# One exponentiated state instead of two: its turned copy by 32 x 32 blocks and DRAM, logits in four column groups

## The chip, the cores and the metric

The kernel runs on 1 core of one Trainium2 chip. The metric is the device time of one execution in microseconds (us); lower is better. All data are fp32.

## The reference

The input x has 8 sequences of 256 tokens of 256 features (2048 tokens). The layer is x + attention(LN(x)) + FFN(LN(x)). The attention works with 16 heads of 128 and, per head, M = 64 states per token:

```
s   = clip(hs @ Ws1.T @ Ws2.T + bs2, -32, 32)      # [token, head, 64]
z   = cumlogsumexp(s, over tokens)
es  = exp(s);  enz = exp(-z)
A   = causal(q @ k.T * scale)                      # q, k with rotary positions
ok  = enz * (A @ es)                               # [token, 64]
qv  = softmax(ok)
W2  = causal((qv * enz) @ es.T)
o   = W2 @ v
out = (rmsnorm(o) * g_norm * silu(g)) @ Wo.T
```

es is thus contracted twice: over tokens in `A @ es` (the logits), and over states in `(qv * enz) @ es.T` (the weights). The FFN unpacks 4-bit weights (2048 x 256 three times) and computes down(gelu(gate) * up).

## The kernel before, in words

The work is cut into 32 steps: 4 groups of 512 tokens (two sequences; `TC` = 4 blocks of 128) times 8 pairs of heads. A step n is a pipeline stage: in loop turn n the kernel makes states, q and k of step n + 1, values, gates, scores, logits and softmax of step n, weights and outputs of step n - 1, and in every second turn `close` (the product with w_o) of steps n - 2 and n - 1. One bank of FFN work (`feeding`) is put in at evenly spread places, 4 or 5 a turn, and decoding of packed FFN weights (24 parts) by the list `DUE`.

The order on TensorE (PE) is written by hand: `POS` gives each piece its place within a turn, `START` other places for turns -1 and 0, `FEED` the stretch in which turn -1 gets FFN work. The pieces call their matmuls at once. What the other engines do with the results is a generator (`chain`) that names its engine and a cost at each `yield`; a planner (`advance`) issues the chains' instructions in the order of its own clocks, lowest `rank` first among equals, and `need` makes it issue all that a piece depends on. So the order on VectorE (DVE), ScalarE (ACT), GpSimd (POOL) and the DMA queue of SyncE (SP) is fixed when the program is built. PSUM has eight banks (`bank`).

Before, `states(n)` makes the states of a head pair twice on PE, in four row groups of 32 partitions (17 of them used: 16 ranks and a row of ones for the bias): four matmuls give [token, state] (tile es, L532), two of 256 columns give [state, token] (tile esT, L537). DVE clips both (L549), ACT exponentiates both (L555), and DVE makes enz from esT by a scan (L560) and a reciprocal (L566). es serves `logits` (L675, a head's 64 states in each of two column groups) and `cross` (L746, es with the values of a sequence's first half); esT serves `weights` (L771). `apply` (L799) puts cross into the outputs' banks.

Some results have to change from [token, feature] to [feature, token]. `turned` does that for ok and the softmax (tile ok to okT) and for the outputs (og to ogT): DVE transposes 32 x 32 blocks (L472), four DMAs on SP write them to a DRAM tile by_way (L476), and one reads them back (L485).

Other lines that are spoken of: rope L579 (PE), L589/L590 (ACT copies z), L592 (DVE), L594/L595 (POOL, tiles z, q and k); values and gates L636; scores L655/L658 with mask L646; ok from the logits' bank L686; maximum L707, exponentials L718, prT L729 (POOL); wt L781; outputs L815, their squares L828, L833, power L837, og L841; close L865; FFN gate L395, up L417, down L442, with L402 to L426 between them; decoding L349, L353, L355; norm L252 to L270; scaling of w_o by the norm's weight L495 (POOL); warm-up matmuls L879.

Of the kernel before, what the change touches and what calls it, by code (L numbers as in the profile page):

```python
# [10 lines left out]
F32 = mybir.dt.float32  # L11
I32 = mybir.dt.int32
# [15 lines left out]
SCALE = DK ** -0.5  # L28
GELU_C = 0.7978845608028654
GELU_A = 0.044715  # L30
WARM = 18


POS = {'scores': (0.053, 0.063),
 'logits': (0.14,),
 'softmax': (0.301,),
 'cross': (0.15,),
 'weights': (0.169,),
 'low': (0.046,),
 'states': (0.167,),  # L40
 'outputs': (0.364, 0.472),
 'close': (0.348, 0.396),
 'rope': (0.197, 0.336, 0.411, 0.543),
 'vg': (0.502, 0.663, 0.838, 0.869)}
START = {-1: {'states': (0.437,), 'rope': (0.128, 0.358, 0.518, 0.588)},
 0: {'vg': (0.0, 0.03, 0.076, 0.214),
     'scores': (0.082, 0.162),
     'states': (0.386,),
     'logits': (0.216,),
     'softmax': (0.433,),  # L50
     'rope': (0.211, 0.24, 0.245, 0.458)}}
FEED = {-1: (0.244, 1.0)}
NORMS = {0: 1, 2: 2, 5: 3}
NORM_AT = (0.204, 0.465)
FIRST = [0.29, 1.5]
LAST = [1.49, 1.82]
DUE = [4, 6, 7, 7, 8, 9, 10, 11, 11, 11, 12, 13, 14, 15, 15, 16, 17, 17, 18, 19, 19, 22, 23, 23, 24]


@with_exitstack  # L60
def layer_kernel(ctx: ExitStack, tc: tile.TileContext, a: dict, out: bass.AP):
# [40 lines left out]
    def S(n):  # L102
        return "s", 0.15 + 0.00088 * n

    def pe(t):

        clock["pe"] += t
# [32 lines left out]
    def new(pool, shape, tag, bufs=1, dtype=F32):  # L140

        users = held.setdefault(tag, [])
        if len(users) >= bufs:
            while any(c in chains for c in users[-bufs]):
                advance()
            floor[0] = max([floor[0]] + [c.at for c in users[-bufs]])
        t = pool.tile(shape, dtype, tag=tag, name=tag, bufs=bufs)
        users.append([])
        at_tag[id(t)] = t, users[-1]
        return t  # L150
# [8 lines left out]
    def chain(gen, *tiles, rank=1, at=0.0):  # L159


        c = Chain()
        c.rank = rank
        c.gen, c.at, c.what = gen, max(clock["pe"] + 0.2, floor[0], at), next(gen)
        floor[0] = 0.0
        chains.append(c)
        for t in tiles:
            at_tag[id(t)][1].append(c)
        return c

    def bank():
        t = new(ps_p, [P, 512], "ps", 8)
        clock["pe"] = max(clock["pe"], floor[0])
        floor[0] = 0.0
        return t
# [8 lines left out]
    nhalf = const.tile([P, TC], F32, tag="nhalf", name="nhalf")  # L184
    turns = const.tile([P, 2, T], F32, tag="turns", name="turns")
    cos, sin = turns[:, 0], turns[:, 1]

    small = const.tile([P, 258], F32, tag="small", name="small")
    w_s1 = small[:, 0:256].rearrange("p (c f) -> p c f", c=2)
# [297 lines left out]
        )  # L487

    def load_wo():
        for h in range(0, H, 4):  # L490
            nc.sync.dma_start(out=w_o[:, h : h + 4, :], in_=a["wo"][:, h : h + 4, :])

    def scale_wo(h):

        nc.gpsimd.tensor_scalar(  # L495
            w_o[:, h : h + 4, :], w_o[:, h : h + 4, :], gw, 0.5, ALU.mult, ALU.mult
        )

    def low_rank(g):

# [16 lines left out]
    def states(n):  # L517

        g, hp = steps[n]
        ms = slice(hp * P, (hp + 1) * P)  # L520
        (rT, c), to = rTs[g], of[n]
        need(c)
        es = to["es"] = new(p2, [P, TC, P], "es", 2)
        esT = to["esT"] = new(p2, [P, G], "esT", 2)

        pss = [bank() for _ in range(4)]
        toks, sts = [rT[32 * r : 32 * r + 17] for r in range(4)], [w_s2[32 * r : 32 * r + 17, ms] for r in range(4)]
        for i in range(2):
            for r, ps in enumerate(pss):
                if r < 2:  # L530
                    k = 2 * r + i
                    nc.tensor.matmul(  # L532
                        ps[:, i * P : (i + 1) * P], lhsT=toks[r][:, k * P : (k + 1) * P],
                        rhs=sts[r], start=True, stop=True,
                    )
                elif i == 0:
                    nc.tensor.matmul(  # L537
                        ps[:, 0:T], lhsT=sts[r], rhs=toks[r][:, (r - 2) * T : (r - 1) * T],
                        start=True, stop=True,
                    )  # L540

        enz = to["enz"] = new(p2, [P, G], "enz", 2)

        def work():
            flat = es.rearrange("p i m -> p (i m)")
            for t, r in ((esT, 2), (flat, 0)):
                yield "v", 0.8
                for k in range(2):
                    nc.vector.tensor_scalar(  # L549
                        t[:, k * T : (k + 1) * T], pss[r + k][:, 0:T], CLAMP, -CLAMP,  # L550
                        ALU.min, ALU.max,
                    )
            for t in (esT, flat):
                yield S(512)
                nc.scalar.activation(t, t, AF.Exp)  # L555
            for b in range(2):
                yield "v", 0.75
                e = esT[:, b * T : (b + 1) * T]

                nc.vector.tensor_tensor_scan(  # L560
                    enz[:, b * T : (b + 1) * T], e, e, 0.0, ALU.add, ALU.max
                )
            for i in range(TC):
                yield "v", 0.93
                r = enz[:, i * P : (i + 1) * P]
                nc.vector.reciprocal(r, r)  # L566

        pe(0.8)
        to["states"] = chain(work(), *pss, es, esT, enz)

    def rope(n, j, which):

# [93 lines left out]
    def logits(n):  # L666

        to = of[n]
        need(to["at", 0][1], to["at", 1][1], to["states"])
        es, enz = to["es"], to["enz"]  # L670
        ps = bank()
        for b in range(2):
            for c, q0 in ((0, 0), (1, P)):
                for j in range(2):
                    nc.tensor.matmul(  # L675
                        ps[j * M : (j + 1) * M, b * T + q0 : (b + 1) * T],
                        lhsT=es[:, 2 * b + c, j * M : (j + 1) * M],
                        rhs=to["at", j][0][b][:, 2 * c * P : 2 * c * P + T - q0],
                        start=c == 0, stop=c == 1,
                    )  # L680
        ok = new(p1, [P, 4, TC, 32], "ok")
        okT = to["okT"] = new(p1, [P, 4, TC, 32], "okT")

        def work():
            yield V(512)
            nc.vector.tensor_tensor(  # L686
                ok.rearrange("p c i k -> p i c k"), ps.rearrange("p (i c k) -> p i c k", i=TC, c=4),
                enz.rearrange("p (i c k) -> p i c k", i=TC, c=4), ALU.mult,
            )
            yield from turned(okT, ok)  # L690

        pe(1.4)
        to["logits"] = chain(work(), ps, ok, okT, enz, rank=0)
# [43 lines left out]
    def cross(n):  # L737


        to = of[n]  # L740
        need(*(to["v", i] for i in (0, 2)))
        es, v = to["es"], to["v"]
        ps = bank()
        for b in range(2):
            for j in range(2):
                nc.tensor.matmul(  # L746
                    ps[j * M : (j + 1) * M, b * DK : (b + 1) * DK],
                    lhsT=es[:, 2 * b, j * M : (j + 1) * M],
                    rhs=v[:, 2 * b, j * DK : (j + 1) * DK], start=True, stop=True,
                )  # L750
        z = new(p1, [P, 2 * DK], "cross")

        def work():
            yield S(256)
            nc.scalar.copy(z, ps[:, 0 : 2 * DK])

        pe(0.55)

        to["cross"] = z, chain(work(), ps, z)
# [96 lines left out]
    def close(n, i):  # L856

        g, hp = steps[n]
        ogT = [of[m]["ogT", j] for m in (n - 1, n) for j in range(2)]
        need(*(c for _, c in ogT))  # L860
        pst = bank()
        ps = pst.rearrange("p (i d) -> p i d", i=2)
        for k in range(2):
            for hh in range(4):
                nc.tensor.matmul(  # L865
                    ps[:, k, :], lhsT=ogT[hh][0][:, i + k],
                    rhs=w_o[:, (hp // 2) * 4 + hh, :], start=hh == 0, stop=hh == 3,
                )
        pe(1.73)
        chain(add_to(g * TC + i, ps), pst)  # L870
# [98 lines left out]
def _layout(x):  # L969
# [11 lines left out]
    def quarters(spread, of):  # L981
# [8 lines left out]
    n = {k: np.asarray(v) for k, v in x.items()}  # L990
    at, ff = "L0_attn_", "L0_ffn_"
    ws1 = n[at + "Ws1"].T.reshape(P, 2, 1, 16)
    ws1 = np.pad(ws1, [(0, 0)] * 3 + [(0, 16)]).repeat(4, 2).reshape(P, 256)
    bias = (np.arange(P) % 32 == 16).astype(np.float32).reshape(P, 1)
    ws2 = np.concatenate([n[at + "Ws2"].T, n[at + "bs2"].reshape(1, H * M)])
    ws2 = np.pad(ws2, [(0, 15), (0, 0)])
    return {
        "x": c(n[at + "hidden_states"].reshape(NG, 4, 4, 32, D).swapaxes(1, 2).reshape(NTOK, D)),
        "wqkvg": pairs([n[at + w] for w in ("Wq", "Wk", "Wv", "Wg")]),
        "wo": c(n[at + "Wo"].T.reshape(H, DK, D).transpose(1, 0, 2)),  # L1000
        "small": c(np.concatenate([ws1, bias, n[at + "g_norm_weight"].reshape(DK, 1)], 1)),
        "ws2": c(np.concatenate([ws2] * 4)),
        "codes": quarters(lambda w: w, "_W_packed"),
        "scales": quarters(lambda w: w.repeat(16, 0), "_scales"),
        "turns": c(np.concatenate([cos, sin], 1)),
# [19 lines left out]
```

## Time and profile before

| | |
|---|---|
| median of 3 runs | 1224.25 us (1223.51 to 1225.16) |
| the profiled execution's own time | 1225.03 us |
| its span | 1223.3 us |
| mean granted TensorE clock | 0.993 |
| DMA | 118.52 MB, 97 GB/s in the mean; the program's queue took 35.1% of 16 engines' span |

The span runs from the first to the last instruction; the rest of the execution's time lies around it. In the profile PE stands for matmuls and PEld for weight loads, which overlap them; an fp32 matmul is recorded as two MATMUL instructions. In the groups by line, the columns are: engine, operation, output <- inputs, shapes, count | busy time and mean ns of one | idle time of the engine just before them, and what ended it. In the list of waits they are: total us, times, longest us.

### The profile page before, as it was taken

The numbers are of one execution on the slowest core, as the hardware profiler recorded it, in microseconds if no ns is written. First come the engines' busy times: TensorE is split into PE (matmuls) and PEld (weight loads), VectorE is DVE, ScalarE is ACT, GpSimd is POOL, SyncE is SP. The second block draws the span as 40 slices with busy tenths as digits, with TensorE's granted clock in tenths as the row PEclk, the third lists the DMA queues.
The fourth block names the chain that finished last, engine by engine and source line by source line (L and its number), as shares of the span: only waits on it lengthen the run. The fifth ranks groups of instructions, "written<-read, shape, count | busy, mean of one in ns | idle before, by whom it ended". The sixth has DMA issues, their size and how long they took to land.

```text
span 1223.3 us, 18297 instructions
## 1 busy us (share of the span) xinstructions
PE 1191.8 (97%) x6076; PEld 841.9 (69%) x6076; DVE 905.0 (74%) x1739; ACT 511.4 (42%) x1641; POOL 483.2 (40%) x439
## 2 busy tenths in 40 slices
PE   9889799999999999999999999999999999999997
PEld 6456576666767667677776677776766767667675
DVE  6978768988477787866877776987776677676743
ACT  3433435435354443534444344444344454443431
POOL 4424544334344343444442344443234443343411
PEclk9989899999999999999999999999999999999999
DMA  5344542343343143333333333423233332334321
GB/s 185 87 121 121 130 112 63 102 129 104 87 104 106 45 117 96 104 96 94 85 90 90 99 104 104 103 56 101 70 104 95 95 80 69 100 98 117 84 76 52
DMA packets 120030, 118.52 MB, mean 97 GB/s; under 512 B 18688, under 2 KB 91520, under 8 KB 119936
## 3 DMA queue, kind: packets, MB, share of 16 engines
q1 hardware_dynamic: 119936, 117.36, 35.1%
q8 instruction: 48, 0.79, 0.3%
q14 instruction: 46, 0.38, 0.1%
HBM read 80.09 MB, written 37.22 MB: 96 GB/s over the span
## 4 chain that ended last, share of the span: by engine, by line
PE 85%; DVE 10%; POOL 2%; ACT 1%; issue 1%; DMA 1%; SPq 0%; DVEq 0%; POOLq 0%
PE ps L579 16%; PE ps L636 16%; PE ps L442 9%; PE ps L865 9%; PE ps L395 8%; PE ps L417 8%; PE ps L815 4%; PE ps L655 4%; PE ps L675 3%; PE ps L771 2%; PE ps L658 2%; DVE enz L566 1%; DVE esT L549 1%; PE ps L746 1%; PE ps L532 1%
## 5 line engine op out<-in xcount | busy, mean ns | idle before, releaser
L594 POOL TENSOR_TENSOR z<-z,turns 128x512 f32<-128x512 f32 x128 | 164.4, 1284 | 242.3 <-ACT z L590 235.6
L579 PE MATMUL ps<-xT,wts 128*128 128x512 f32 x512 | 241.8, 599 | 5.7 <-DVE t L410 1.6
L636 PE MATMUL ps<-wts,xT 128*128 128x256 f32 x1024 | 234.7, 379 | 1.0 <-DVE k L592 1.0
L636 PEld LDWEIGHTS ps<-wts,xT 128*128 128x128 f32 x1024 | 193.5, 190 | 52.3 <-issue 24.2
L579 PEld LDWEIGHTS ps<-xT,wts 128*128 128x128 f32 x512 | 93.6, 190 | 91.5 <-issue 77.2
L442 PE MATMUL ps<-w_down,inter 128*128 128x256 f32 x512 | 121.0, 390 | 8.8 <-DVE inter L426 4.2
L404 POOL TENSOR_SCALAR t<-t 128x512 f32<-128x512 f32 x64 | 40.0, 624 | 209.8 <-ACT t L402 207.8
L417 PE MATMUL ps<-xT,w_up 128*128 128x512 f32 x256 | 121.6, 597 | 0.0
L395 PE MATMUL ps<-xT,w_gate 128*128 128x512 f32 x256 | 120.7, 594 | 0.5 <-DVE sgate L624 0.5
L718 ACT ACTIVATE ok<-okT,mx 128x64 f32<-128x64 f32 x256 | 85.6, 337 | 81.5 <-DVE mx L712 80.3
L442 PEld LDWEIGHTS ps<-w_down,inter 128*128 128x128 f32 x512 | 98.9, 196 | 28.9 <-DVE inter L426 5.6
L589 ACT COPY z<-ps 64x512 f32<-64x512 f32 x128 | 74.6, 583 | 104.5 <-PE ps L579 98.7
L865 PE MATMUL ps<-w_o,ogT 128*128 128x256 f32 x512 | 115.6, 379 | 0.0
L595 POOL TENSOR_TENSOR q<-q,z 128x512 f32<-128x512 f32 x64 | 81.8, 1278 | 82.8 <-DVE q L592 59.8
L865 PEld LDWEIGHTS ps<-w_o,ogT 128*128 128x128 f32 x512 | 96.7, 190 | 21.3 <-issue 9.3
L566 DVE RECIPROCAL enz<-enz 128x128 f32<-128x128 f32 x128 | 108.1, 905 | 0.0
L370 DVE TENSOR_TENSOR res<-ps,res 128x512 f32<-128x512 f32 x64 | 43.8, 685 | 78.4 <-PE ps L442 42.5
L841 DVE SCALAR_TENSOR_TENSOR og<-ps,ss,sgate 128x128 f32<-128x128 f32 x256 | 73.5, 342 | 37.7 <-POOL ss L837 37.7
L837 POOL TENSOR_TENSOR ss<-ss,nhalf 128x4 f32<-128x4 f32 x64 | 64.9, 1017 | 68.6 <-DVE ss L833 66.5
L595 POOL TENSOR_TENSOR k<-k,z 128x512 f32<-128x512 f32 x64 | 82.9, 1295 | 20.9 <-DVE k L592 15.7
L408 ACT ACTIVATE t<-t 128x512 f32<-128x512 f32 x64 | 40.2, 629 | 121.2 <-DVE t L406 121.1
L646 DVE TENSOR_TENSOR at<-ps,mask 128x384 f32<-128x384 f32 x128 | 66.1, 551 | 32.7 <-PE ps L658 31.8
(80 smaller groups left out, 1919.7 us busy)
## 6 DMA issues: line engine op xcount, KB each, us to landing
wts<-in_wqkvg_dram SPq DMA_DIRECT2D x64, 512.0 KB, 4.4
by_way<-ok SPq DMA_DIRECT2D x256, 64.0 KB, 1.8
okT<-by_way SPq DMA_DIRECT2D x64, 256.0 KB, 2.7
by_way<-og SPq DMA_DIRECT2D x256, 64.0 KB, 2.0
ogT<-by_way SPq DMA_DIRECT2D x64, 256.0 KB, 4.0
pk<-in_codes_dram SPq DMA_DIRECT2D x12, 256.0 KB, 3.7
sc<-in_scales_dram SPq DMA_DIRECT2D x12, 256.0 KB, 3.6
w_o<-in_wo_dram SPq DMA_DIRECT2D x4, 512.0 KB, 5.6
```

The costliest lines, as they stand in the source:

```text
L395: nc.tensor.matmul(pg, lhsT=w_gate[:, c, ns], rhs=xT[:, c, gs], start=c == 0, stop=c == 1)
L417: nc.tensor.matmul(pu, lhsT=w_up[:, c, ns], rhs=xT[:, c, gs], start=c == 0, stop=c == 1)
L442: nc.tensor.matmul(ps[:, k, :], lhsT=inter[g, n][0][:, (i + k) * P : (i + k + 1) * P], rhs=w_dn[:, n, :], start=n == 2 * q, stop=n == 2 * ...
L566: nc.vector.reciprocal(r, r)
L579: nc.tensor.matmul(ps, lhsT=w[:, c, :], rhs=xT[:, c, g * G : (g + 1) * G], start=c == 0, stop=c == 1)
L589: nc.scalar.copy(z[0:64], pv[64:128])
L594: nc.gpsimd.tensor_tensor(z, z, sin_b, ALU.mult)
L595: nc.gpsimd.tensor_tensor(y, y, z, ALU.add)
L636: nc.tensor.matmul(ps[:, k, :], lhsT=xT[:, c, tt], rhs=w[:, which, c, :], start=c == 0, stop=c == 1,)
L718: nc.scalar.activation(pr[:, js, i, :], okT[:, js, i, :], AF.Exp, bias=mx[:, k : k + 1], scale=SCALE, accum_out=sm[:, k : k + 1],)
L841: nc.vector.scalar_tensor_tensor(og[:, :, k, :], po[:, k, :].rearrange("p (c k) -> p c k", c=4), ss[:, k : k + 1], sg[:, k, j * DK : (j + ...
L865: nc.tensor.matmul(ps[:, k, :], lhsT=ogT[hh][0][:, i + k], rhs=w_o[:, (hp // 2) * 4 + hh, :], start=hh == 0, stop=hh == 3,)
```

## The change

`states` makes only [state, token], with two matmuls in two row halves of 64 partitions (17 used in each). ScalarE writes the exponential twice, once in blocks of 32 into a tile `u` (shared with decoding) and once in place; the first goes through `turned` to es. `logits` and `cross` take es in four column groups of 32 states. `w_o` is scaled by chains of rank 2 that the planner places, and `close` needs them. Three warm-up matmuls fewer are run, and places and due times differ. Cut to its core:

```diff
-WARM = 18
-POS = {'scores': (0.053, 0.063),
+WARM = 15
+POS = {'scores': (0, 0.089),
- 'softmax': (0.301,),
+ 'softmax': (0.366,),
- 'outputs': (0.364, 0.472),
- 'close': (0.348, 0.396),
- 'rope': (0.197, 0.336, 0.411, 0.543),
- 'vg': (0.502, 0.663, 0.838, 0.869)}
-START = {-1: {'states': (0.437,), 'rope': (0.128, 0.358, 0.518, 0.588)},
+ 'outputs': (0.319, 0.427),
+ 'close': (0.396, 0.407),
+ 'rope': (0.178, 0.317, 0.392, 0.524),
+ 'vg': (0.502, 0.64, 0.838, 0.869)}
+START = {-1: {'states': (0.488,), 'rope': (0.221, 0.424, 0.53, 0.684)},
...
-     'states': (0.386,),
+     'states': (0.445,),
-     'rope': (0.211, 0.24, 0.245, 0.458)}}
-FEED = {-1: (0.244, 1.0)}
+     'rope': (0.24, 0.245, 0.249, 0.458)}}
+FEED = {-1: (0.055, 1.0)}
-LAST = [1.49, 1.82]
-DUE = [4, 6, 7, 7, 8, 9, 10, ..., 19, 19, 22, 23, 23, 24]
+LAST = [1.51, 1.82]
+DUE = [4, 6, 6, 7, 9, 9, 10, ..., 19, 19, 23, 23, 23, 24]
...
     def scale_wo(h):
-        nc.gpsimd.tensor_scalar(
-            w_o[:, h : h + 4, :], w_o[:, h : h + 4, :], gw, 0.5, ALU.mult, ALU.mult
-        )
+        def work():
+            yield "g", 1.15
+            nc.gpsimd.tensor_scalar(
+                w_o[:, h : h + 4, :], w_o[:, h : h + 4, :], gw, 0.5, ALU.mult, ALU.mult
+            )
+        scaled.append(chain(work(), rank=2, at=landed["wo"]))
...
-        pss = [bank() for _ in range(4)]
...
+        pss = [bank() for _ in range(2)]
+        for b, ps in enumerate(pss):
+            rows = slice(64 * b, 64 * b + 64)
+            nc.tensor.matmul(
+                ps[:, 0:T], lhsT=w_s2[rows, ms], rhs=rT[rows, b * T : (b + 1) * T],
+                start=True, stop=True,
+            )
...
+        u = new(de, [P, 2, CH], "u", 2, I32)
+        eb = u.bitcast(F32).rearrange("p k (x i y) -> p (k x) i y", i=TC, y=32)
+        es = to["es"] = new(p2, [P, 4, TC, 32], "es", 2)
+        def clipped():
+            yield "v", 0.8
+            for b in range(2):
+                nc.vector.tensor_scalar(
+                    esT[:, b * T : (b + 1) * T], pss[b][:, 0:T], CLAMP, -CLAMP, ALU.min, ALU.max
+                )
+            yield S(512)
+            nc.scalar.activation(
+                eb.rearrange("p c i k -> p i c k"),
+                esT.rearrange("p (i c k) -> p i c k", i=TC, c=4), AF.Exp,
+            )
+        def swapped():
+            yield first
+            yield from turned(es, eb)
+        def summed():
+            yield first
+            yield S(512)
+            nc.scalar.activation(esT, esT, AF.Exp)
...
-        pe(0.8)
-        to["states"] = chain(work(), *pss, es, esT, enz)
+        pe(0.65)
+        first = chain(clipped(), *pss, esT, u)
+        to["es_at"] = chain(swapped(), es, u)
+        to["states"] = chain(summed(), esT, enz)
...
         # logits; cross in the same way
-                for j in range(2):
+                for r in range(4):
                     nc.tensor.matmul(
-                        ps[j * M : (j + 1) * M, b * T + q0 : (b + 1) * T],
-                        lhsT=es[:, 2 * b + c, j * M : (j + 1) * M],
-                        rhs=to["at", j][0][b][:, 2 * c * P : 2 * c * P + T - q0],
+                        ps[32 * r : 32 * (r + 1), b * T + q0 : (b + 1) * T],
+                        lhsT=es[:, r, 2 * b + c, :],
+                        rhs=to["at", r // 2][0][b][:, 2 * c * P : 2 * c * P + T - q0],
...
         # close
-        need(*(c for _, c in ogT))
+        need(*(c for _, c in ogT), *scaled)
```

More of the change, by code (lines that the diff above doesn't have):

```diff
@@ L55 @@
 FIRST = [0.29, 1.5]
-LAST = [1.49, 1.82]
-DUE = [4, 6, 7, 7, 8, 9, 10, 11, 11, 11, 12, 13, 14, 15, 15, 16, 17, 17, 18, 19, 19, 22, 23, 23, 24]
+LAST = [1.51, 1.82]
+DUE = [4, 6, 6, 7, 9, 9, 10, 11, 11, 11, 12, 13, 14, 15, 15, 16, 17, 17, 18, 19, 19, 23, 23, 23, 24]
 @with_exitstack
@@ L489, in load_wo @@
     def load_wo():
+        loads("wo", 2048)
         for h in range(0, H, 4):
@@ L493, in scale_wo @@
     def scale_wo(h):
-        nc.gpsimd.tensor_scalar(
-            w_o[:, h : h + 4, :], w_o[:, h : h + 4, :], gw, 0.5, ALU.mult, ALU.mult
-        )
+        def work():
[4 more added lines that the diff above has]
+        scaled.append(chain(work(), rank=2, at=landed["wo"]))
+    scaled = []
     def low_rank(g):
@@ L522, in states @@
         need(c)
-        es = to["es"] = new(p2, [P, TC, P], "es", 2)
         esT = to["esT"] = new(p2, [P, G], "esT", 2)
-        pss = [bank() for _ in range(4)]
[L527 to L540, printed above, removed]
@@ L542, in states @@
-        enz = to["enz"] = new(p2, [P, G], "enz", 2)
[L544 to L555, printed above, removed]
+        pss = [bank() for _ in range(2)]
@@ L668, in logits @@
         to = of[n]
-        need(to["at", 0][1], to["at", 1][1], to["states"])
+        need(to["at", 0][1], to["at", 1][1], to["states"], to["es_at"])
         es, enz = to["es"], to["enz"]
@@ L740, in cross @@
         to = of[n]
-        need(*(to["v", i] for i in (0, 2)))
+        need(to["es_at"], *(to["v", i] for i in (0, 2)))
         es, v = to["es"], to["v"]
@@ L744, in cross @@
         for b in range(2):
-            for j in range(2):
+            for r in range(4):
+                j = r // 2
                 nc.tensor.matmul(
-                    ps[j * M : (j + 1) * M, b * DK : (b + 1) * DK],
-                    lhsT=es[:, 2 * b, j * M : (j + 1) * M],
+                    ps[32 * r : 32 * (r + 1), b * DK : (b + 1) * DK],
+                    lhsT=es[:, r, 2 * b, :],
                     rhs=v[:, 2 * b, j * DK : (j + 1) * DK], start=True, stop=True,
@@ L992, in _layout @@
     ws1 = n[at + "Ws1"].T.reshape(P, 2, 1, 16)
-    ws1 = np.pad(ws1, [(0, 0)] * 3 + [(0, 16)]).repeat(4, 2).reshape(P, 256)
-    bias = (np.arange(P) % 32 == 16).astype(np.float32).reshape(P, 1)
+    ws1 = np.pad(ws1, [(0, 0)] * 3 + [(0, 48)]).repeat(2, 2).reshape(P, 256)
+    bias = (np.arange(P) % 64 == 16).astype(np.float32).reshape(P, 1)
     ws2 = np.concatenate([n[at + "Ws2"].T, n[at + "bs2"].reshape(1, H * M)])
-    ws2 = np.pad(ws2, [(0, 15), (0, 0)])
+    ws2 = np.pad(ws2, [(0, 47), (0, 0)])
     return {
@@ L1001, in _layout @@
         "small": c(np.concatenate([ws1, bias, n[at + "g_norm_weight"].reshape(DK, 1)], 1)),
-        "ws2": c(np.concatenate([ws2] * 4)),
+        "ws2": c(np.concatenate([ws2] * 2)),
         "codes": quarters(lambda w: w, "_W_packed"),
```

## The prediction

> **What bounds the kernel now.** I read the head of the page first, then PE's waits, the stretches of the start, one step's timeline on PE, and last the groups by form for single prices.
>
> ```profile
> span 1223.3 us, 18297 instructions
> PE 1191.8 (97%) x6076; PEld 841.9 (69%) x6076; DVE 905.0 (74%) x1739; ACT 511.4 (42%) x1641; POOL 483.2 (40%) x439
> ```
>
> TensorE is busy for 97% of the span, so a change pays where it shortens PE's own sequence or one of the few waits in it. The stretches (columns: length, then PE, PEld, DVE, ACT, POOL busy, granted clock, DMA share, GB/s) show where those lie:
>
> ```profile
> 20.00:40.00 20.00, 18.97 (x83) 12.85 (x82) 19.79 (x35) 5.79 (x11) 8.17 (x9) 1.00 0.24 79
> 40.00:60.00 20.00, 15.46 (x54) 7.80 (x53) 19.39 (x41) 9.20 (x27) 10.12 (x10) 1.00 0.38 105
> 60.00:80.00 20.00, 15.29 (x93) 10.91 (x93) 13.97 (x27) 3.72 (x7) 1.75 (x2) 0.83 0.32 73
> 120.00:145.00 25.00, 18.65 (x66) 11.89 (x66) 17.69 (x43) 11.26 (x37) 16.59 (x16) 0.86 0.57 147
> 145.00:180.00 35.00, 34.89 (x186) 26.82 (x183) 23.88 (x45) 13.93 (x48) 14.03 (x12) 1.00 0.35 91
> ```
>
> From 20 to 60 us VectorE is full (39.2 of 40 us) and PE waits for it. Two long PE stalls end at 66 us (4.1 us, on a decoded weight) and at 138.5 us (5.3 us, on POOL k). Each is followed by a lowered clock: 0.83 over 20 us and 0.86 over 25 us, some 3.4 us each. From 145 us on PE is full and DVE has a third of its time free. Every later step looks like this one (start, length, line; 16 records of a line are 8 matmuls, since an fp32 matmul is recorded twice):
>
> ```profile
> 144.10 1.52 PE L675 MATMUL ps<-at,es 128*64 128x256 f32 x16
> 145.45 0.61 PE L746 MATMUL ps<-v,es 128*64 128x128 f32 x8
> 145.98 0.38 PE L532 MATMUL ps<-w_s,rT 17*128 17x128 f32 x2
> ...
> 146.63 1.16 PE L771 MATMUL ps<-prT,esT 64*128 64x128 f32 x16
> 147.62 0.61 PE L799 MATMUL ps<-cross,prT 64*128 64x128 f32 x8
> 148.34 1.98 PE L579 MATMUL ps<-xT,wts 128*128 128x512 f32 x4
> ```
>
> Start to start, the logits take 1.35 us, cross 0.53, states 0.65, weights 0.99, apply 0.72. Step 31, which has no states and no rope behind apply, gives two prices without them:
>
> ```profile
> 1155.29 0.61 PE L746 MATMUL ps<-v,es 128*64 128x128 f32 x8
> 1155.83 1.16 PE L771 MATMUL ps<-prT,esT 64*128 64x128 f32 x16
> 1156.82 0.61 PE L799 MATMUL ps<-cross,prT 64*128 64x128 f32 x8
> 1157.36 1.98 PE L395 MATMUL ps<-xT,w_gate 128*128 128x512 f32 x4
> ```
>
> Here apply takes 0.54, so the 0.72 ahead of a rope holds 0.18 us of waiting. The weight loads name its cause:
>
> ```profile
> L579 PEld LDWEIGHTS ps<-xT,wts 128*128 128x128 f32 x512 | 93.6, 190 | 91.5 <-issue 77.2 <-DVE esT L549 7.2 <-DVE t L410 1.8
> PE ps L799 <- DVE esT L549: 1.7, 5, 0.3
> ```
>
> Rope and apply want a PSUM bank that the clip of the states still reads.
>
> **The change part by part.** *States on PE.* Six matmuls in four row groups become two of 256 columns in two row halves. Sixteen 256-wide records of L636 or L865 start 3.45 us before the next group, so one costs 0.216 us; two rounds in which both halves run together cost 0.43. That halves do run together is seen in L771: 16 records of 64 rows take 0.99 us, 0.06 each, where eight full-height 128-wide records of L815 take 0.89. The block is also in the same row mode as the weights behind it. The 0.65 includes a gap of 0.2 between the last states start (146.42) and the first weights start (146.63), where rounds in one mode are 0.11 apart, so one change of mode goes. I take 0.44: 0.21 saved in the 30 steps where weights follow states, 6.3 us. Bounds: 0.54 (the gap stays; 3.3 us saved) and 0.86 (halves one after the other; 6.3 lost).
>
> *Banks.* Logits, cross, states, weights and apply draw 10 of 8 banks before, 8 after, so rope no longer needs a bank of the states. 30 × 0.18 = 5.4 us and the 1.7 us of L799 go. What is late next is the bank of the logits, whose product (L686) ends at 146.35, 2 us before rope. Bounds: 0 to 7.1 saved.
>
> *Four column groups.* Logits go from 8 to 16 matmuls, cross from 4 to 8, with 32 weight columns each. No row shows four column groups. The nearest rows: two column groups cost no more than one matmul (cross, 8 records of 128 columns in pairs, 0.53 with its mode gap; L815 needs 0.89 for 8 unpaired), and four row groups start 8 records within 146.20 to 146.43, rounds 0.11 apart as well. I take 3 ns more for each of the 12 rounds of a step, the difference between rounds of row groups (112 ns) and of column pairs (109 ns) in their starts: 32 × 12 × 3 ns = 1.2 us. Bounds: 0, and two rounds for one (the rival below). The Trainium skill, "TensorE: Matmul & The Clock Gate", section "Measured speedup vs the span model", gives about 4 ns for each further tile; two more tiles in 12 rounds of 32 steps would make 3.1 us, an estimate by that page, and the forecast 1216.
>
> *VectorE and ScalarE.* 64 clips of es (L549, 413 ns: 23.8 us less, the pair overlapping) go; 32 block transposes at the 703 ns of L472 come, 22.5 us. Net zero; hidden from 145 us on by the free third of DVE. The two exponentials stay at 630 ns each. The one for es goes first, so enz is 0.6 us later; it is ready 20 us or more ahead of the logits, 5.7 us for head pair 0.
>
> *The way by DRAM.* Per step SP issues four writes and one read more. By the og rows: 1.8 us to issue the writes, 2.0 to land, 0.3 to issue the read, 4.0 to land. From the states' start: clip and exponential by about 2.6 us, transpose 0.7, then 8.1: es is there after 12 us. The logits that read it start 28 to 40 us after the states, 22 us for pair 0. So the copy itself costs nothing; the cover would have to shrink by 10 us. The queue is what it passes: on SP the read of okT (about 6.7 us after the logits) and the writes of og stand behind it, up to 3.5 us later. Behind okT stand maximum, exponentials, prT and the weights of the next step. Softmax is also placed 0.065 of a 36 us step later, 2.3 us. From the starts of L771 and ends of L729 the slack there is 2.6 us at 437 us, 3.3 at 295, 3.9 at 75, 4 to 6 in three more, above that elsewhere. I charge 1 us; bounds 0 and 9.6 (all six steps, 5.8 us late).
>
> *The start.* Three warm-up matmuls fewer are 1.15 us of 6.9, but the first transposes wait for z at 7.25 us instead of 7.92, and DVE is full until 68 us behind them: 0, bounds −0.6 and 0.6. The new order (a rope behind the first logits, the feed and low rank ahead of ropes) changes what waits in a stretch that DVE sets: 0, bounds −3 and +7.5, one new stall of 4 us with its 3.4 us of clock. One decode part (two of 754, 622, 930 to 1,403 ns: 3.1 to 3.5 us of DVE) moves from step 1 to step 2, where the 5.3 us stall lies. Against it, the scaling of w_o (2.22 us on POOL at 133.63, straight ahead of z and k) becomes a chain of lowest rank; z had been ready since 134.85 and starts at 135.80, so it held k up by 0.95 us. I take 0, bounds −8.7 (stall and clock go) and +3.5.
>
> *Places.* Both scores still follow one another ahead of the same feed; outputs come ahead of close, where wt is ready 5.5 us or more before use and close lasted 3.45: at least 2 us stay. Cost 0, 0.7 a product if that is gone.
>
> Sum: −6.3 − 5.4 − 1.7 + 1.2 + 1.0 = −11.2. The profiled execution took 1225.03 us (span 1223.3 and 1.7 around it), 0.8 above the median of the three runs, 1224.25. 1225.0 − 11.2 gives **1214**. What a measurement of this kernel can tell from no change is about 0.2%, 2.4 us.
>
> **The rivals.**
>
> *A round of four column groups is longer than a pair (slower).* Its place is L675 and L746. Logits rounds take four times 0.216 and four times 0.109, cross four times 0.109: 1.74 us a step. If four run as two pairs, that comes again: 32 × 1.74 = 55.6 and 1225 − 12.4 + 55.6 + 1 = 1269. It decides from rounds longer by a fifth (11.2 / 55.6) on. For it: no row has four. Against: neither pairs of columns nor four row groups cost anything. 0.10, the price between the ends included. The Trainium skill, same page and section, has four row tiles at 3.07 times one tile, not 4; by that a round would take 1.30 times one matmul, 0.30 × 55.6 = 16.7, and the whole 1229, an estimate by that page. The trace's four row groups, one round per 0.11 us like single matmuls, disagree with it.
>
> *The start gets worse.* One stall of 4 to 5 us more, with the half clock after it, gives 1214 + 7.5 = 1221.5; two give 1229. For: DVE at 99%, a decode part moved into the step with the longest stall, scores of pair 0 with 1.8 us of slack for the second head. Against: less POOL work in front of k. 0.11.
>
> *The freed PE time comes back as waits* (prT late by the SP queue and the later place, bank waits on other readers): 1225 − 6.3 + 1.2 + 4 = 1224, no change. Against: DVE, ACT and POOL are far from full after 145 us. 0.07.
>
> *More is gained:* the stall at 138 us goes with its clock, 1214 − 8.7 = 1205. 0.06.
>
> **How the numbers follow.** The forecast has 0.66. The range 1206 to 1230 takes in its bounds and the start's rival up to two stalls; left out are longer rounds and the best case, about 0.15. Faster: forecast, best case and half of the start's rival, 0.77. The same: the third rival and a little of the second, 0.08. Slower: the first and the rest, 0.15.
>
> **What would show it.** Right: L532/L537 replaced by 4 records some 0.44 us ahead of L771; apply to rope 0.54; logits still 1.35 to 1.4 and cross 0.53 to 0.56; no wait of PE for the okT or es transfers. Wrong: logits near 2.6 us; L675 waiting for a DMA into es; L771 waiting for prT; clock below 1 at other places than 66 and 138 us.

## The result and the profile after

The changed kernel takes 1212.88 us (median of 4; before 1223.88 beside it): a ratio of 0.9904, 95% interval 0.9886 to 0.9922. Beside three other kernels later it took 1212.2, ratio 0.9914 (0.9901 to 0.9928). The forecast was 1214. The profiled execution took 1210.61 us.

The head of the changed kernel's page:

```profile
span 1208.8 us, 19563 instructions
PE 1175.7 (97%) x6582; PEld 828.8 (69%) x6582; DVE 887.8 (73%) x1707; ACT 515.0 (43%) x1641; POOL 485.8 (40%) x439
```

Its view of stretches in the start (columns as before):

```profile
20.00:40.00 20.00, 18.20 (x97) 12.44 (x96) 18.07 (x37) 6.22 (x12) 6.89 (x7) 1.00 0.36 104
40.00:60.00 20.00, 15.18 (x42) 6.83 (x40) 19.10 (x35) 8.91 (x27) 11.21 (x10) 1.00 0.51 132
60.00:80.00 20.00, 15.05 (x117) 11.69 (x118) 16.11 (x30) 4.02 (x7) 3.71 (x3) 0.83 0.34 75
120.00:145.00 25.00, 17.70 (x81) 11.33 (x83) 18.57 (x47) 11.08 (x37) 16.26 (x16) 0.86 0.67 167
145.00:180.00 35.00, 35.00 (x191) 26.82 (x184) 26.41 (x49) 14.26 (x48) 14.44 (x12) 1.00 0.33 85
```

PE is as full as before. Its busy time is 16.1 us shorter, the span 14.5 us, since the time in which PE stands still has grown from 31.5 to 33.1 us. The start is much like the old one: DVE full from 40 to 60 us, PE short of work, the clock at 0.83 and 0.86 in the same two stretches. One step on PE (start, length, line) shows where the time came from:

```profile
143.82 1.51 PE L689 MATMUL ps<-at,es 128*32 128x256 f32 x32
145.14 0.62 PE L761 MATMUL ps<-v,es 128*32 128x128 f32 x16
145.69 0.70 PE L536 MATMUL ps<-rT,w_s 64*128 64x256 f32 x4
146.22 1.06 PE L786 MATMUL ps<-prT,esT 64*128 64x128 f32 x16
147.12 0.61 PE L814 MATMUL ps<-cross,prT 64*128 64x128 f32 x8
147.66 1.98 PE L593 MATMUL ps<-xT,wts 128*128 128x512 f32 x4
```

The logits of step 3 start at 143.82 us instead of 144.10: three steps into the kernel, nearly nothing is gained. From there on each step is shorter. Start to start: logits 1.32 us (1.35 before), cross 0.55 (0.53), states 0.53 (0.65), weights 0.90 (0.99), apply 0.54 (0.72). That is 0.4 us a step. The weight loads of rope, which had waited 7.2 us in total for the clip of the states, are left with 1.7, and the wait of apply's matmuls is gone from PE's list of waits. The groups by line, with what ended the idle time, and then the list of waits (total us, count, longest):

```profile
L593 PEld LDWEIGHTS ps<-xT,wts 128*128 128x128 f32 x512 | 93.4, 190 | 87.3 <-issue 77.9 <-DVE esT L551 1.7 <-DVE u L473 1.2
```

```profile
PE ps L669 <- POOL k L609: 17.1, 5, 7.7
PE ps L443 <- DVE inter L427: 3.4, 2, 3.1
PE ps L786 <- POOL prT L743: 2.2, 1, 2.2
```

The long waits are those of the scores for POOL's k (L669), now 17.1 us. Before, the line was:

```profile
PE ps L655 <- POOL k L595: 8.7, 3, 5.3
```

They lie in the start, where a wait for a decoded weight (4.1 us) went in turn. One wait of 2.2 us of the weights for prT is new.

### The profile page after: what moved, and what is told of

Read it like the earlier page. It is cut to its first block, busy times and chain, and to the rows that moved or that the text cites. A ratio compares the mean times of both kernels' runs of the same rounds, so it can differ in the third digit from the quotient of the medians.

```text
span 1208.8 us, 19563 instructions
## 1 busy us (share of the span) xinstructions
PE 1175.7 (97%) x6582; PEld 828.8 (69%) x6582; DVE 887.8 (73%) x1707; ACT 515.0 (43%) x1641; POOL 485.8 (40%) x439
## 4 chain that ended last, share of the span: by engine, by line
PE 86%; DVE 7%; POOL 2%; issue 1%; DMA 1%; ACT 1%; SPq 0%; DVEq 0%; POOLq 0%
PE ps L593 16%; PE ps L650 15%; PE ps L880 9%; PE ps L443 9%; PE ps L396 8%; PE ps L418 8%; PE ps L669 4%; PE ps L830 4%; PE ps L689 4%; PE ps L786 2%; PE ps L672 2%; PE ps L536 2%; PE ps L814 1%; PE ps L761 1%; DVE enz L578 1%
## 5 line engine op out<-in xcount | busy, mean ns | idle before, releaser
L608 POOL TENSOR_TENSOR z<-z,turns 128x512 f32<-128x512 f32 x128 | 167.9, 1312 | 221.1 <-ACT z L604 219.6
L443 PE MATMUL ps<-w_down,inter 128*128 128x256 f32 x512 | 116.5, 380 | 3.4 <-DVE inter L427 3.4
L880 PE MATMUL ps<-w_o,ogT 128*128 128x256 f32 x512 | 113.1, 379 | 0.0
L443 PEld LDWEIGHTS ps<-w_down,inter 128*128 128x128 f32 x512 | 96.4, 191 | 21.2 <-DVE inter L427 4.8
L669 PE MATMUL ps<-q,k 128*128 128x256 f32 x256 | 79.2, 392 | 17.5 <-POOL k L609 17.1
```

What stands on the lines that cost most here:

```text
L443: nc.tensor.matmul(ps[:, k, :], lhsT=inter[g, n][0][:, (i + k) * P : (i + k + 1) * P], rhs=w_dn[:, n, :], start=n == 2 * q, stop=n == 2 * ...
L608: nc.gpsimd.tensor_tensor(z, z, sin_b, ALU.mult)
L669: nc.tensor.matmul(ps[:, 0:T], lhsT=k[:, b, 0:P], rhs=q[:, b, :], start=True, stop=True)
L880: nc.tensor.matmul(ps[:, k, :], lhsT=ogT[hh][0][:, i + k], rhs=w_o[:, (hp // 2) * 4 + hh, :], start=hh == 0, stop=hh == 3,)
```

## The experiments

**The schedule alone.** The kernel before, with the new places, due times, warm-up count and w_o chains, but the states still made twice.

```diff
-POS, START, FEED, LAST, DUE, WARM, scale_wo of before
+POS, START, FEED, LAST, DUE, WARM, scale_wo of the changed kernel
```

> The kernel before with only the new places, due times, warm-up count and the w_o chains; states are still made twice in four row groups. Theory (the gain is PE time in the states block and bank waits behind it): no gain, 1222 to 1228 us, with states still 0.64, weights 0.99 and apply 0.72 us a step; differences only in the stalls ahead of 145 us. Rival (the new places make the gain): 1210 to 1216.

1229.41 us, ratio 1.0052 (1.0036 to 1.0068): half a per cent slower. One of its steps:

```profile
516.05 0.38 PE L539 MATMUL ps<-w_s,rT 17*128 17x128 f32 x2
...
516.70 1.16 PE L778 MATMUL ps<-prT,esT 64*128 64x128 f32 x16
517.69 0.61 PE L806 MATMUL ps<-cross,prT 64*128 64x128 f32 x8
518.41 3.70 PE L586 MATMUL ps<-xT,wts 128*128 128x512 f32 x8
```

States 0.65, weights 0.99, apply 0.72: the blocks are untouched, and the new places bring nothing by themselves. They came out slower than the theory's range. The profiled execution was the slowest of six (1234.01 us). In its start scores wait 7.3 us and then a decoded weight 2.5, where the kernel before waits 3.0 and 4.1; at 258.7 us a wait of 3.0 us for xT is new. Which of the new places causes which wait was not taken apart.

**The states alone.** The changed kernel with all the old numbers and the old scaling of w_o.

```diff
-POS, START, FEED, LAST, DUE, WARM, scale_wo of the changed kernel
+POS, START, FEED, LAST, DUE, WARM, scale_wo of before
```

> The changed kernel with the old places, due times, warm-up count and w_o scaling. Theory: all of the gain, 1208 to 1216 us: states 0.54, weights 0.89, apply 0.54 us a step. Rival (the places make it): 1221 to 1227 although those blocks are shorter, the difference coming back as waits for es, prT or a bank.

1212.53 us, ratio 0.9911 (0.9898 to 0.9923): the whole gain, as the theory had it, with blocks of 0.54, 0.89 and 0.54 us. The 2.2 us wait of the weights for prT is not in its list. In the step in which it falls (near 219 us) prT is ready 5.1 us ahead of the weights in the kernel before, and 4.1 here; with the schedule alone PE waits 0.4 us for it, in the changed kernel 2.2. So the new places took up most of that slack and the way of es by DRAM one to two microseconds, and the wait comes from both together.

**Four banks.** The same PE time, but four banks of states to clip.

```diff
-        pss = [bank() for _ in range(2)]
-        for b, ps in enumerate(pss): ...         # 256 columns into ps
+        pss = [bank() for _ in range(4)]
+        for i in range(2):
+            for b in range(2): ...               # 128 columns into pss[2 * b + i]
-            for b in range(2): clip 256 columns of pss[b]
+            for k in range(4): clip 128 columns of pss[k]
```

> The changed kernel with the states spread over four banks: four matmuls of 128 columns in two row halves (two rounds of 0.11 us twice, the same PE time) and four clips of 128 columns. Theory (rope and apply waited for a bank of the states): apply comes back from 0.54 towards 0.72 us a step and waits of rope or apply on the clip return, 1214 to 1221 us. Rival (the wait went because the clip or the change of mode went, whatever the number of banks): apply stays at 0.54, 1210 to 1215.

1222.32 us, ratio 0.9991 (0.998 to 1.0001): nearly all of the gain is lost, a little more than the theory's range. In the groups of weight loads, and then in PE's list of waits, the clip is back:

```profile
L815 PEld LDWEIGHTS ps<-cross,prT 64*128 64x128 f32 x256 | 19.8, 188 | 3.1 <-DVE esT L552 3.1
L594 PEld LDWEIGHTS ps<-xT,wts 128*128 128x128 f32 x512 | 93.3, 190 | 88.2 <-issue 76.0 <-DVE esT L552 3.6 <-DVE wt L797 1.9
```

```profile
PE ps L815 <- DVE esT L552: 1.7, 7, 0.4
```

Added up over the 32 steps from start to start, apply takes 24.2 us against 17.4, weights 30.1 against 28.8: 8.1 of the 10 us. A usual step has apply at 0.59 us and not at 0.72; most of the loss lies in eleven steps, in which apply takes 0.81 to 1.45 us. The clips were also cut in four (0.88 us together, against 0.74 for two), and this execution had more stretches at half clock; what these two add was not separated from the number of banks.

**Rows of 32.** The two matmuls of the states in row groups of 32, everything else the same.

```diff
-            rows = slice(64 * b, 64 * b + 64)
+            rows = slice(32 * b, 32 * b + 32)
```

(The padding of the small weights is that of before.)

> The changed kernel with the two matmuls of the states in row groups of 32 partitions (0 to 31, 32 to 63) instead of row halves of 64; the same number of matmuls, banks and clips. Theory (part of the saving is one change of row mode fewer between states and weights): states and weights together come back from 1.43 to 1.6 us a step, 30 x 0.1 to 0.2, so 1214 to 1219 us. Rival (the saving is the four matmuls fewer alone): they stay at 1.43, 1210 to 1215.

1219.91 us, ratio 0.9969 (0.9956 to 0.9981), 0.9 us above the theory's range. One step:

```profile
509.11 0.70 PE L536 MATMUL ps<-rT,w_s 32*128 32x256 f32 x4
509.74 1.16 PE L786 MATMUL ps<-prT,esT 64*128 64x128 f32 x16
510.74 0.61 PE L814 MATMUL ps<-cross,prT 64*128 64x128 f32 x8
511.28 3.70 PE L593 MATMUL ps<-xT,wts 128*128 128x512 f32 x8
```

States 0.63, weights 1.00: 1.63 us, as before the change (1.64), although two matmuls stand where six stood. Apply stays at 0.54, since the banks are still two. So the 6 us of this part are the change of row mode between states and weights, and the four matmuls left out are worth nothing: in the prediction's timeline of the kernel before, [token, state] and [state, token] start side by side (145.98 and 146.00 us). The Trainium skill, "TensorEngine Tiling (Array Packing)", section "Key Properties", says that a change of tiling mode drains the array; the trace agrees, and prices it at 0.2 us here.

**Two column groups at a time.** The same matmuls of logits and cross in another order.

```diff
-        for b in range(2):
+        for pair, b in (((0, 1), 0), ((0, 1), 1), ((2, 3), 0), ((2, 3), 1)):
...
-                for r in range(4):
+                for r in pair:
```

> The changed kernel with the same 16 and 8 matmuls of logits and cross, ordered so that column groups 0 and 1 do all their work before 2 and 3; so only two run at a time. Theory (a round of four costs as much as a pair only because all four run at once): logits 2.6 and cross 1.0 us a step, 1210 + 55 = 1266 us. Rival (the matmuls with 32 columns are simply shorter): logits stay near 1.3, 1210 to 1216.

1233.04 us, a single execution: neither number. 20 us more than the changed kernel show that the four do run at once there. That it is 20 and not 55 has a reason in the timeline:

```profile
146.46 1.07 PE L689 MATMUL ps<-at,es 128*32 128x256 f32 x18
147.16 0.41 PE L761 MATMUL ps<-v,es 128*32 128x128 f32 x4
147.36 0.39 PE L689 MATMUL ps<-at,es 128*32 128x256 f32 x2
147.40 0.39 PE L761 MATMUL ps<-v,es 128*32 128x128 f32 x4
147.58 0.39 PE L689 MATMUL ps<-at,es 128*32 128x128 f32 x4
147.80 0.61 PE L761 MATMUL ps<-v,es 128*32 128x128 f32 x8
```

Cross (L761) comes after all logits (L689) in the program, yet its first matmuls start at 147.16 us, before logits at 147.36 and 147.58. The profile does not name the groups, but by the program's order the early ones should be cross on groups 0 and 1, and the late ones logits on groups 2 and 3. Matmuls of two column groups overtook those of the other two, so the pairs ran partly side by side: logits and cross took 2.55 us a step, against 1.87 in the changed kernel. 32 x 0.68 = 22 us.

**Two trips by DRAM.** The way of es doubled, DMAs alone.

```diff
             yield from turned(es, eb)
+            # in words: four more writes of eb to another by_way, one more read into es
```

> The changed kernel with the way of es by DRAM gone twice: after the first read four more writes and one more read of the same blocks, 160 transfers more in all. Theory (the copy lies in the 13 us and more between its read and the logits): no PE wait for es, within 3 us of the changed kernel, 1211 to 1216. Rival (SP's queue is on the path to the weights by okT and prT, whose slack is down to 0.1 to 1.4 us in some steps): waits of the weights for prT, 1217 to 1228.

1214.86 us, ratio 0.993 (0.9914 to 0.9946). Its interval overlaps that of the changed kernel, whose medians are 2.0 and 2.7 us lower, so a second trip costs little or nothing. PE's list of waits has none for es: the copy lies inside the cover. The wait of the weights for prT, the rival's, is 2.9 us there instead of 2.2.

**Filled stalls.** The states alone, with matmuls of ones ahead of three scores that wait for k.

```diff
+FILL = {(1, 0): 8, (1, 1): 24, (3, 1): 16}
...
+        if (n, j) in FILL:        # in scores(n, j)
+            ps = bank()
+            for _ in range(FILL[n, j]):
+                nc.tensor.matmul(ps[:, 0:P], lhsT=ones, rhs=ones, start=True, stop=True)
```

> The states alone on the old places (it ran at 1212.5 us), and ahead of three scores that wait for k (head pair 1, both heads, and pair 3, second head) 8, 24 and 16 matmuls of ones into a bank that nobody reads, 0.22 us each, to keep PE working where it would stand still for 2.0, 6.6 and 5.3 us. Theory (each long stall costs a second time, by a half clock of 7 to 14 us after it): the half clock near 54 and 136 us goes, 20.5 us at half, so up to 10 us less: 1202 to 1208. Rival (the clock falls for another reason, or PE's idle time just follows the filling): 1211 to 1215, or above by the filling, 1220.

1209.2 us, ratio 0.9883 (0.9868 to 0.9898): better than the changed kernel, but 3.3 us under the states alone instead of up to 10.

**With w_o scaled together** as well:

```diff
-                put_at(0.3 + 0.04 * h, scale_wo, h)
+                put_at(0.3 + 0.001 * h, scale_wo, h)
```

> As the filled kernel, and the four scalings of w_o put together at 0.3 of turn 2, where POOL is idle for over 10 us, instead of two of them straight ahead of the z and k that PE waits for near 137 us. Theory: that k is ready 0.95 us sooner, the wait shrinks from 5.3 to 4.3 us less the filling, 0 to 1 us less than the filled kernel. Rival (k is late by DVE alone): the same as the filled kernel.

1208.68 us, ratio 0.988 (0.9866 to 0.9895). The wait of the second scores of pair 3 shrank from 1.7 to 0.9 us, as expected; the total is too close to the filled kernel's to tell.

**The changed kernel and the best one on one chip, and filling on the kernel before.**

> The changed kernel as it is, beside the next two on one chip: 1210 to 1215 us. It is the measure for them, and shows whether the half clock falls at the same two places in another execution.

> The kernel that ran at 1208.7 us (states alone on the old places, filled stalls, w_o scaled together), unchanged. Theory (the half clock after stalls and the order of POOL are worth 3 to 5 us on top of the states): 1207 to 1210, 2 to 5 us under the changed kernel beside it. Rival (the difference was one between chips): within 1 us of it.

> The kernel before with the filling and the w_o scalings together, nothing else. Theory (filling is independent of the states): 3 to 4 us less than before, 1219 to 1221; with the 11 us of the states this makes up the best kernel. Its blocks stay at 0.64 (states), 0.99 and 0.72. Rival (the states' part is what the filled kernel gains from): 1223 to 1225, as before.

The changed kernel 1212.2 us (0.9914; 0.9901 to 0.9928), the best one 1208.43 (0.9886; 0.9871 to 0.9901), the filled kernel before 1218.37 (0.9963; 0.995 to 0.9975). Filling and the order of w_o give 4.1 us on the old kernel and 3.8 on the new, so they are independent of the states. (The best kernel has the old places, the changed one the new; the states alone, on the old places, ran at 1212.53.) The stretches 60 to 80 and 120 to 145 us, first of the states alone, then of the best kernel:

```profile
60.00:80.00 20.00, 16.77 (x122) 13.15 (x123) 15.59 (x26) 4.02 (x7) 4.42 (x4) 0.80 0.38 82
120.00:145.00 25.00, 17.73 (x101) 11.49 (x99) 16.48 (x39) 10.40 (x33) 15.86 (x15) 0.86 0.58 148
```

```profile
60.00:80.00 20.00, 17.27 (x135) 12.66 (x134) 17.04 (x28) 4.02 (x7) 4.49 (x4) 1.00 0.41 95
120.00:145.00 25.00, 22.61 (x167) 17.39 (x168) 20.09 (x46) 11.64 (x33) 11.32 (x11) 1.00 0.62 157
```

The clock (the third number from the end) is full where it was 0.80 and 0.86. Only part of that is time: a slow clock costs nothing while PE waits for k, and counts from the end of the wait. In the states alone the waits end at 63.2 and 136.9 us, and the granted clock is 0.50 from there to 67.8 and to 142.9. That is 10.6 us at half clock, worth 5.3 us; the filled kernel keeps 3.4 us at half clock after a wait that ends at 63.0 us, worth 1.7. The estimate from these numbers is 3.6 us, and 3.3 were measured.

## Why the prediction was right

*The total.* 1214 forecast, 1212.9 and 1212.2 measured. The mechanisms held, some with other sizes; that the total is so close is in part luck. The terms below add up to 14 us and not 11.2: banks saved 2.7 us more, the column groups did not cost their 1.2, and the prT wait cost 1.2 more. The two profiled executions lie 14.4 us apart, but that of the changed kernel was the fastest of its four, and the medians lie 11.0 apart. The second profiled execution of the changed kernel (1212.70 us) is at the logits of step 3 at 144.83 us, a microsecond later than the first; the rest of the difference was not traced.

*States on PE:* 6.3 us forecast. States and weights together went from 1.64 to 1.43 us, 30 x 0.21 = 6.3. The reason given, one change of row mode fewer, is shown by the rows of 32: put the change of mode back and the whole amount is back. But the amount does not lie where the prediction put it. It had states fall to 0.44 us and held weights at 0.99; states fell to 0.53, its bound for a gap that stays, and weights to 0.90. About half of what a change of mode costs thus falls into the block behind it. Two misses of about 0.1 us a step cancel, so the sum is in part luck.

*Banks:* 7.1 us forecast, and this term was too small. From start to start, added over the steps, apply goes from 27.2 to 17.4 us: 9.8. The prediction counted 1.7 us for the five steps in which apply itself waits, from the gaps in PE's list (0.3 us each). One of these steps in the kernel before:

```profile
188.65 0.72 PE L771 MATMUL ps<-prT,esT 64*128 64x128 f32 x10
189.21 0.38 PE L799 MATMUL ps<-cross,prT 64*128 64x128 f32 x2
189.93 0.71 PE L799 MATMUL ps<-cross,prT 64*128 64x128 f32 x6 [0.34 <-DVE esT L549]
```

Apply starts at 189.21 us and goes on at 189.93; rope starts at 190.57. The block takes 1.36 us instead of 0.72, 0.64 more where the list has 0.34. In five more steps weights and apply mix, and take 1.97 to 2.21 us together instead of 1.71. The four banks bring the wait for the clip back, so the banks are its cause, with the reservation made there.

The prediction did not ask why the clip is so late. In the kernel before it waits itself:

```profile
147.86 0.76 DVE L549 TENSOR_SCALAR esT<-ps 128x256 f32<-128x256 f32 x2 [0.29 <-PE ps L771]
```

esT has two buffers, so the clip for step n + 1 writes the one that the weights (L771) of step n - 1 read in the same turn. DVE waited for them in 22 steps, 10.6 us in all, and in the changed kernel still does in 8 (5.6 us), where little on PE hangs on it (1.7 us of rope's weight loads). A third buffer of esT in the kernel before, another way to free the banks sooner, was not tried.

*Four column groups:* 1.2 us forecast as a cost. They cost nothing: logits and cross together went from 1.88 to 1.87 us in the step shown, and the logits' groups on PE are no longer than before with twice the records. The kernel before, then the changed one:

```profile
L675 PE MATMUL ps<-at,es 128*64 128x256 f32 x256 | 41.1, 392 | 0.0
L675 PE MATMUL ps<-at,es 128*64 128x128 f32 x256 | 26.1, 273 | 0.0
```

```profile
L689 PE MATMUL ps<-at,es 128*32 128x256 f32 x512 | 40.2, 385 | 0.0
L689 PE MATMUL ps<-at,es 128*32 128x128 f32 x512 | 25.8, 273 | 0.0
```

The Trainium skill, "TensorE: Matmul & The Clock Gate", section "Measured speedup vs the span model", would have added about 4 ns for each further tile; in this stream nothing of it is seen, and the forecast by it, 1216, was farther off. The forecast by the 3.07 times that the same section of the Trainium skill has for four row tiles, 1229, is farther still.

*The way by DRAM:* nothing, as forecast. In the changed kernel the read of es is issued 13.5 us ahead of the first logits and 18 us or more ahead of all others, and it lands after 2.8.

*Softmax later:* 1.0 us charged; one wait of 2.2 us came. It fell not in the step with the least slack (437 us) but near 219 us, one of the steps for which the prediction had read 4 to 6 us. The new places made most of it and the SP queue a part, as the states alone, the schedule alone and the two trips show.

*The start:* taken as no change, with bounds on both sides. The logits of step 3 start 0.3 us sooner. The decode part and the chains of w_o did not move the 5.3 us wait (5.2 after): POOL still scales two parts of w_o straight ahead of z and k, at 133.50 us instead of 133.63.

```profile
132.25 1.27 POOL L609 TENSOR_TENSOR q<-q,z 128x512 f32<-128x512 f32 x1
133.50 2.21 POOL L499 TENSOR_SCALAR w_o<-w_o,small 128x1024 f32<-128x1024 f32 x2
135.67 1.26 POOL L608 TENSOR_TENSOR z<-z,turns 128x512 f32<-128x512 f32 x1
```

The rank in the planner decides only among chains that can begin at the same time. POOL was free at 133.50 us, and the z that it then held up was ready only at 134.72, 0.95 us before its turn. Moving the place did help (the wait of 1.7 us shrank to 0.9).

*The rivals:* longer rounds of column groups did not come. Freed time came back as waits only in small part (the 2.2 us for prT). The start's rival did not come in the changed kernel, though on the old one the new places cost 6 us; why they cost nothing that can be told on the changed kernel is open. Of the signs of being wrong, two appeared once each: the wait for prT, and, in the second profiled execution of the changed kernel, a clock of 0.90 between 40 and 60 us.

## What to carry to other kernels

Where PE is full, count the changes of tiling mode and the PSUM banks drawn in a burst before counting matmuls, and ask what keeps the reader of a late bank: here one mode change fewer and two banks fewer made the gain, and four matmuls fewer made none. A change that comes with a new schedule should be run in its two halves; the schedule here was not part of the gain. Work put into an unavoidable wait of PE kept the clock up here, and was worth the time at half clock that follows the wait, not the time inside it.

## What the runs showed of the hardware that was not expected

Matmuls of different column groups were not kept in program order: cross started at 147.16 us, before logits at 147.36 and 147.58 that precede it. Row halves did the same in the kernel before: a matmul of apply (L799) started at 1126.04 us, and one of the weights (L771), which precede it, at 1126.14. A wait for a bank inside a run of small matmuls cost more than its gap: a block of 0.72 us took 1.36 with a gap of 0.34. The stretches at half clock vary between executions of one kernel: the changed kernel's two profiled executions had 6.8 and 13.7 us of it near 60 us, and took 1210.6 and 1212.7 us.
